# The first block's value weights: eight load slots, an earlier first split, three low halves on GpSimd, and later low halves of the values

## The chip, the cores and the metric

The kernel runs on one core of one Trainium2 chip. The metric is the device time of one execution in microseconds; of several executions the median counts. In the views, PE is TensorE's matmul row, PEld its weight loads, DVE VectorE, ACT ScalarE, POOL GpSimd, and SP the engine whose queue issues most DMAs.

## The reference

A transformer layer over two sequences of 2048 tokens with 2048 channels: layer norm, single-head attention with 512 features, and a routed low-rank feed-forward part, both added to the input.

```python
xn = layernorm(x)                                   # per token, over 2048 channels
q, k, v = split(xn @ Wqkv + bqkv)                   # 512 features each
att = softmax(q @ k.T / sqrt(512)) @ v @ Wo + bo
s = (xn @ Wq_w.T) @ keys.T                          # router, 16 dimensions, 64 experts
gate = softmax over the 16 largest of s, 0 elsewhere
z = (xn @ A_w.T).reshape(64, 8) * gate[:, None]     # 8 columns for each expert
out = x + att + (z @ B_w.T) * 2
```

All is float32.

## The kernel before

**Numbers in two halves.** The operands of the products are of type fp32r. Every one is split in two: the high half is a cast copy (`split_hi`, a cast on ScalarE, line 121), the low half is what is missing (`split_lo`, a subtraction on VectorE, line 124). `product` (line 129) then does three matmuls: low token half by high weight half, high by low, high by high.

**Blocks.** The 4096 tokens are eight blocks of 512, each of four token tiles of 128 rows. The first block is made by `first_block`, before anything else; this change is in it alone. Other blocks and the attention follow, and are not touched.

**What the first block does.** For each token tile t it loads 128 rows (`load`, line 340), takes the row statistics on VectorE (`normal`: lines 200, 203, then nm at 348 and, in `rstd`, ve at 193 and a power on GpSimd at 194 that gives rs), scales the rows (`scale`: three quarters on VectorE at 356, one on ScalarE at 360 and 361), transposes them on TensorE (`turn`, line 370, 16 transposes in four groups, each group into one accumulator), and splits the transposed group into high and low halves (xh, lines 121 and 124). Then come the products with the value weights. The values (with the 16 router columns) are 528 columns wide and are made in two halves h of 264 columns. The weights of one half come in eight pieces of 128 by 528 numbers (two channel chunks of 264), each of 264 KB, loaded at line 270 into a slot ws, and split into wh. One token tile with one piece takes six matmuls, of 128 by 264.

**The order.** In the first half, the products go tile by tile: 36 matmuls of tile 0 (pieces 1 to 6), transposes of tile 1, tile 0's other 12 and 48 of tile 1, transposes of tile 2, 48, transposes of tile 3, 48. In the second half they go piece by piece, each with all four tiles, which is 24 matmuls for a piece. Between these, `values_out` splits each tile's sum into vs (a cast on ScalarE, a subtraction on VectorE that reads the accumulator) and stores it (line 163, through `flush`).

**What sets the order.** Each engine runs its instructions in one order that is fixed when the program is built, by a scheduler. `behind(keys)` puts what is inside it after the last instruction that was noted under these names ("row" is the last row or token operation of VectorE). A `Ring` gives out named buffers in turn, and an instruction that fills one waits until the former content has been read. Here matter: `r_ws` (four slots h0 to h3 for loaded value weights), `r_mb` (B25, B26), `r_wu` (seven slots, B32 and B33 the last two, for query, key and feed-forward weights), `r_ev` (three slots, for vs among others), and the seven accumulators `acc` in PSUM, which are given to transposed groups and to sums alike.

In the first block, `pieces(n)` loads and splits pieces until n are there:

```python
        turn(0, 0, 2)
        pieces(2)
        turn(0, 2, 4)
        pieces(4)
        load(1, 1024)
```

and two more are asked for at the start of tile 0's products, and the last two in the midst of them.

Of the kernel before, what the change touches and what calls it, by code (L numbers as in the profile page):

```python
# [8 lines left out]
F32 = mybir.dt.float32  # L9
# [7 lines left out]
P = 128  # L17
# [10 lines left out]
VH = (D + RD) // 2  # L28
# [5 lines left out]
def raw(ap):  # L34
    return ap.bitcast(F32)
# [27 lines left out]
def attn_ffn_kernel(ctx: ExitStack, tc, x, xT, wq, wv, wob, bqk, bv, bo, keysT, out):  # L63
    nc = tc.nc
# [10 lines left out]
    sb = ctx.enter_context(tc.tile_pool(name="sb", bufs=1))  # L75
# [5 lines left out]
    def big(*js):  # L81
        return Ring(sb, *(f"B{j}" for j in js))
# [4 lines left out]
    def half(*js):  # L87
        return Ring(sb, *(f"H{j}" for j in js))

    def mid(*js):  # L90
        return Ring(sb, *(f"h{j}" for j in js))
# [6 lines left out]
    def acc():  # L98
        return psum.tile([P, T], F32, name="acc", tag="acc", bufs=7)
# [11 lines left out]
    def behind(*keys):  # L111

        ctx_ = ExitStack()
        for k in keys:
            ctx_.enter_context(tc.issue_after(last[k].ins))
        return ctx_

    def split_hi(hi, src):  # L120
        return nc.scalar.copy(hi, src)  # L121

    def split_lo(lo, src, hi, eng=None):
        return (eng or nc.vector).tensor_tensor(lo, src, raw(hi), ALU.subtract)  # L124
# [33 lines left out]
    def store(dst, src):  # L158
        pending.append((dst, src))
# [10 lines left out]
    r_ev = big(27, 28, 29)  # L170
# [3 lines left out]
    r_ws = mid(0, 1, 2, 3)  # L174
# [21 lines left out]
    def row_stats(mv, xs, parts, st):  # L196

        for xt in xs:
            for h in range(xt.shape[1] // 512):
                nc.vector.bn_stats(st[:, parts, :], xt[:, h * 512 : (h + 1) * 512])  # L200
                parts += 1
        if parts == 4:
            nc.vector.bn_aggr(mv, st)
        return parts
# [60 lines left out]
            xn.append(xh)  # L265
        return xn

    def weights(src, shape, eng=None, queue=None):
        ws = r_ws([P, *shape], F32, "ws")
        issued = (queue or nc.sync).dma_start(ws, src)  # L270
        if queue is None:
            last["sp"] = issued
        wh = r_wh([P, 2, *shape], FR, "wh")
        last["hi"] = split_hi(wh[:, 0], ws)
        last["dve"] = split_lo(wh[:, 1], ws, wh[:, 0], eng)
        return wh

    def values_out(i, t, h, r, qr, ps, u=None):

        n0 = RD if h == 0 else 0  # L280
        at = 0 if h == 0 else VH - RD
        vs = r([P, 2, VH], FR, "vs")
        if u is None:
            v = ps
            if h == 0:
                nc.scalar.copy(qr[:, t, :RD], ps[:, :RD])
        else:
            v = raw(vs[:, 1, :])
            nc.vector.tensor_tensor(v[:, n0:], ps[:, n0:VH], u[:, n0:], ALU.add)
        last["ev"] = split_hi(vs[:, 0, n0:], v[:, n0:VH])  # L290
        split_lo(vs[:, 1, n0:], v[:, n0:VH], vs[:, 0, n0:])
        store(v_d[i][t][:, :, at : at + VH - n0], raw(vs[:, :, n0:]))

    def wv_piece(h, c2, eng=None, queue=None):
        ch, cc = divmod(2 * c2, HC)
        return weights(wv[h, ch, :, cc : cc + 2, :], [2, VH], eng, queue)

    def router_in():
        qr = const.tile([P, NT, 32], F32, name="qr", bufs=1)
# [26 lines left out]
    def first_block():  # L326


        xs0 = [r_xs, r_xs, r_xs] + [big(j) for j in range(16, 21)]
        xn = [r_xh([P, 2, T], FR, "xh") for c in range(NCH)]  # L330
        rows, mv = {}, const.tile([P, NT, 2], F32, name="mv", bufs=2)
        rs = const.tile([P, NT], F32, name="rs")
        nm = const.tile([P, NT], F32, name="nm")

        def load(t, cols):
            rows[t] = [xs0[2 * t + c]([P, 1024], F32, "xs") for c in range(2)]
            for c in range(2):
                for h in range(1024 // cols):
                    a = h * cols
                    (nc.scalar if t == 0 and c else nc.sync).dma_start(  # L340
                        rows[t][c][:, a : a + cols],
                        x[t * P : (t + 1) * P, c * 1024 + a : c * 1024 + a + cols],
                    )

        def normal(t):
            st = const.tile([P, 4, 6], F32, name="st6", bufs=2)
            row_stats(mv[:, t, :], rows[t], 0, st)
            last["nm"] = nc.vector.tensor_scalar(nm[:, t : t + 1], mv[:, t, 0:1], -1.0, None, ALU.mult)
            rstd(rs[:, t : t + 1], mv[:, t, 1:2], 1)

        def scale(t):
            for n in range(4):
                c, h = divmod(n, 2)
                v = rows[t][c][:, h * 512 : (h + 1) * 512]
                if n < 3:
                    last["row"] = nc.vector.tensor_scalar(
                        v, v, mv[:, t, 0:1], rs[:, t : t + 1], ALU.subtract, ALU.mult
                    )
                else:
                    nc.scalar.activation(v, v, AF.Identity, bias=nm[:, t : t + 1])  # L360
                    last["mul"] = nc.scalar.mul(v, v, rs[:, t : t + 1])

        def turn(t, g0=0, g1=NCH // 4):
            sl = slice(t * P, (t + 1) * P)
            for g in range(g0, g1):
                pt = acc()
                for j in range(4):
                    c = 4 * g + j
                    k = (c % 8) * P
                    nc.tensor.transpose(pt[:, j * P : (j + 1) * P], rows[t][c // 8][:, k : k + P], ident)  # L370
                for part in range(2):
                    for j in range(4):
                        hi, lo = (xn[4 * g + j][:, a, sl] for a in range(2))
                        pj = pt[:, j * P : (j + 1) * P]
                        if part == 0:
                            split_hi(hi, pj)
                        else:
                            last["row"] = split_lo(lo, pj, hi)

        def piece(c2, h, eng=None, queue=None):  # L380
            return wv_piece(h, c2, eng, queue)

        def mul(ps, wh, t, c2):
            sl = slice(t * P, (t + 1) * P)
            for cc in range(2):
                c = 2 * c2 + cc
                product(
                    ps[:, :VH], lambda a: xn[c][:, a, sl], lambda b: wh[:, b, cc, :],
                    c == 0, c == NCH - 1,
                )  # L390

        N2 = NCH // 2
        warm = half(0)([P, T], mybir.dt.bfloat16, "warm")
        nc.vector.memset(warm, 0.0)
        pw = misc()
        for j in range(26):
            nc.tensor.matmul(pw, warm[:, :P], warm, start=True, stop=True)
        load(0, 512)
        normal(0)
        scale(0)  # L400

        wh = []

        def pieces(n):
            with behind("row", "nm", "mul"):
                while len(wh) < n:
                    wh.append(piece(len(wh), 0))

        turn(0, 0, 2)
        pieces(2)  # L410
        turn(0, 2, 4)
        pieces(4)
        load(1, 1024)
        ps = [acc() for t in range(NT)]
        for t in range(NT):
            if t + 1 < NT:
                with behind("row"):
                    normal(t + 1)
            if t == 0:
                pieces(6)  # L420
                load(2, 1024)
            for c2 in range(N2):
                if t + 1 < NT and c2 == 2:
                    scale(t + 1)
                if t == 0 and c2 == 4:
                    pieces(N2)
                    load(3, 1024)
                    constants()
                if t + 1 < NT and c2 == 6:
                    with behind("pe"):  # L430
                        turn(t + 1)
                mul(ps[t], wh[c2], t, c2)
        qr = router_in()
        for t in range(NT):
            values_out(0, t, 0, r_ev, qr, ps[t])
        flush()
        ps = [acc() for t in range(NT)]
        for c2 in range(N2):
            w = piece(c2, 1)
            for t in range(NT):  # L440
                mul(ps[t], w, t, c2)
        for t in range(NT):
            values_out(0, t, 1, r_ev, qr, ps[t])
        return xn, qr
# [120 lines left out]
    def value_sums(m, w):  # L565
# [21 lines left out]
    pieces = [  # L587
        (j, ph, it, g)
        for j in PAIRS for ph in PHASES for it in ITEMS[ph] for g in range(2 if it == "V" else 1)
    ]  # L590
# [386 lines left out]
    xn, qr = first_block()  # L977
    tile_of = lambda fp, fh: ND * (fp // 2) + 2 * fh + fp % 2
    for i in range(2):
        if i:  # L980
            s2 = stats_steps(2, r_xs, 1024, mbs)
            qr = values(i, xn, s2)
# [54 lines left out]
    r_ev = big(27, 28, 29, 9)  # L1037
# [544 lines left out]
    for q in range(2 * NG):  # L1582
# [4 lines left out]
        for n, step in enumerate(STEPS):  # L1587
# [7 lines left out]
            for t in range(NA):  # L1595
                ps = multiply(q, step, t, bank.get(t) if step == "P2" else None)
# [58 lines left out]
```

## Time and profile before

| what | value |
|---|---|
| three runs | 2624.99, 2626.7, 2631.52 us; median 2626.7 |
| profiled execution: its own time | 2629.96 us |
| its span in the profile | 2628.2 us |
| TensorE's granted clock, mean | 0.997 |
| first block: loads of value weights, one piece | 264 KB, 3.8 us from issue to landing (median of 20) |
| first block: loads of rows, half a tile | 512 KB, 8.7 us (median of 6) |
| VectorE: low half of a weight piece, 128 by 528 | 0.70 us |
| VectorE: low half of a transposed chunk, 128 by 128 | 0.28 us, one each 0.2 us |
| ScalarE: high half of a weight piece | 0.62 to 0.83 us |
| VectorE: statistics of a tile, four operations | 2.46 us |
| TensorE: 16 transposes | 2.0 us |

A row of the timeline gives the start in the span, the length, the engine, the line of the kernel, the operation with out<-in, the shape and how many were merged; in brackets the time for which the engine stood idle just before, and what ended that. Instructions of one engine overlap at their ends, so several in a row start closer together than their lengths say. A row "min/median/max" gives durations in ns. In a row of the windows, the stretch and its length come first, then the busy time of each engine.

### The profile page before, as it was taken

To read this page: it belongs to the slowest core of one execution; us is meant where nothing else is said; L and a number is where in the kernel's file an instruction comes from. 1 tells how busy PE (TensorE), PEld (TensorE's weight loads), DVE (VectorE), ACT (ScalarE), POOL (GpSimd) and SP (SyncE) were. 2 spreads that over 40 slices of the span, in tenths; PEclk is the share of its full clock that TensorE was granted. 3 is DMA by queue.
4 is the path that set the end of the run, shared out by engine and by line. 5 is a ranking of instruction groups with operands and counts; after the bars stand their busy time and mean duration, and the time that the engine had idled before them with its cause. 6 is when DMAs were issued, how large, how long until landed. Compare 5 with 4: busy or idle time off the path is not lost. (4 is left out here: it accounts for less than half of the span.)

```text
span 2628.2 us, 34501 instructions
## 1 busy us (share of the span) xinstructions
PE 2592.6 (99%) x12692; PEld 2186.3 (83%) x12692; DVE 1919.4 (73%) x2698; ACT 909.8 (35%) x1345; POOL 516.1 (20%) x315
## 2 busy tenths in 40 slices
PE   8999999999999999999989999999999999999999
PEld 7889888888888888888877877878888888888887
DVE  7557639867878677776758859678598776797675
ACT  4323223323332333343435436344364222332221
POOL 1311420000000000000000000000000765566654
PEclk9999999999999999999999999999999999999999
DMA  6667875668447683576999798799788544565542
GB/s 235 232 248 261 284 262 186 211 211 278 153 136 226 214 274 124 177 257 226 310 305 326 253 329 268 257 331 321 251 294 296 175 164 161 183 217 176 177 162 103
DMA packets 328954, 608.09 MB, mean 231 GB/s; under 512 B 27928, under 2 KB 150864, under 8 KB 328784
## 3 DMA queue, kind: packets, MB, share of 16 engines
q1 hardware_dynamic: 315824, 575.99, 64.9%
q10 hardware_dynamic: 12960, 29.89, 3.4%
q8 instruction: 100, 1.64, 0.3%
q14 instruction: 70, 0.57, 0.1%
HBM read 450.42 MB, written 155.35 MB: 230 GB/s over the span
## 5 line engine op out<-in xcount | busy, mean ns | idle before, releaser
L129 PE MATMUL acc<-t,pw 128*128 128x512 f32 x3024 | 694.0, 390 | 1.6 <-DVE pw L124 1.5
L129 PEld LDWEIGHTS acc<-t,pw 128*128 128x128 f32 x3024 | 565.3, 188 | 119.7 <-DVE pw L124 2.5
L1406 PE MATMUL acc<-wb,s 128*128 128x512 f32 x2688 | 609.4, 389 | 0.0
L1406 PEld LDWEIGHTS acc<-wb,s 128*128 128x128 f32 x2688 | 504.5, 188 | 104.8
L1390 POOL TENSOR_TENSOR xo<-xo,bo_bc 128x512 f32<-128x512 f32 x128 | 205.6, 1613 | 906.4 <-DMA vt<-v_d 606.2
L129 PE MATMUL acc<-ph,vt 128*128 128x512 f32 x1536 | 378.6, 391 | 4.5 <-DVE ot L1255 2.5
L1129 PE MATMUL acc<-qt,kt 128*128 128x512 f32 x1344 | 338.4, 394 | 14.3 <-ACT acc L1112 7.4
L129 PEld LDWEIGHTS acc<-ph,vt 128*128 128x128 f32 x1536 | 287.7, 188 | 68.5 <-DVE ot L1255 4.1
L1129 PEld LDWEIGHTS acc<-qt,kt 128*128 128x128 f32 x1344 | 253.1, 190 | 73.7 <-ACT acc L1112 8.3
L121 ACT CAST pw<-pw 128x1024 fp32r<-128x1024 f32 (+1 forms) x168 | 177.6, 1058 | 324.8 <-PE acc L129 240.9
L129 PE MATMUL acc<-xh,wh 128*128 128x512 f32 x1152 | 263.7, 390 | 0.0
L124 DVE TENSOR_TENSOR pw<-pw 128x1024 fp32r<-128x1024 f32 (+1 forms) x168 | 214.7, 1278 | 64.9 <-ACT pw L121 63.5
L129 PEld LDWEIGHTS acc<-xh,wh 128*128 128x128 f32 x1152 | 215.6, 188 | 44.9
L129 PEld LDWEIGHTS acc<-pw,t 128*128 128x128 f32 x2016 | 245.8, 188 | 1.3
L129 PE MATMUL acc<-pw,t 128*128 128x264 f32 x2016 | 246.4, 283 | 0.0
L121 ACT CAST s<-xz 128x1024 fp32r<-128x1024 f32 x112 | 118.0, 1054 | 368.7 <-PE acc L1406 285.8
L124 DVE TENSOR_TENSOR s<-xz,s 128x1024 fp32r<-128x1024 f32 x112 | 175.4, 1568 | 41.6 <-ACT s L121 41.6
L124 DVE TENSOR_TENSOR wh<-wu,wh 128x512 fp32r<-128x512 f32 x96 | 83.6, 888 | 99.0 <-ACT wh L121 99.0
L519 POOL TENSOR_TENSOR zt<-zt,g 128x512 f32<-128x512 f32 x24 | 38.9, 1630 | 503.3 <-DMA g<-gd 272.4
L121 ACT CAST t<-xq 128x1024 fp32r<-128x1024 f32 x84 | 88.3, 1052 | 103.5 <-PE acc L129 44.8
L124 DVE TENSOR_TENSOR t<-xq,t 128x1024 fp32r<-128x1024 f32 x84 | 108.2, 1292 | 20.6 <-ACT t L121 20.1
L1395 DVE TENSOR_TENSOR xo<-xo,acc 128x512 f32<-128x512 f32 x128 | 86.8, 679 | 49.1 <-PE acc L1406 22.3
(168 smaller groups left out, 2463.2 us busy)
## 6 DMA issues: line engine op xcount, KB each, us to landing
vt<-v_d SPq DMA_DIRECT2D x128, 512.0 KB, 5.3
kt<-kp_d SPq DMA_DIRECT2D x224, 256.0 KB, 5.8
pw<-sq_d SPq DMA_DIRECT2D x72, 512.0 KB, 4.0
xo<-in_x SPq DMA_DIRECT2D x128, 256.0 KB, 3.4
xz<-oz_d SPq DMA_DIRECT2D x64, 512.0 KB, 4.8
out_y<-xo SPq DMA_DIRECT2D x128, 256.0 KB, 2.3
pw<-in_wq SPq DMA_DIRECT2D x54, 512.0 KB, 4.4
wu<-in_wq SPq DMA_DIRECT2D x48, 512.0 KB, 5.9
```

What stands on the lines that cost most here:

```text
L121: return nc.scalar.copy(hi, src)
L124: return (eng or nc.vector).tensor_tensor(lo, src, raw(hi), ALU.subtract)
L129: last["pe"] = nc.tensor.matmul(ps, st(a_), mv(b_), start=first and n == 0, stop=end and n == 2)
L519: nc.gpsimd.tensor_tensor(zt, zt, gx[n], ALU.mult)
L1129: last["pe"] = nc.tensor.matmul(ps, st[:, d, a, :], mv[c][:, d, :], start=not more and d == 0 and i == 0, stop=d == 1 and i == 2, skip_gro ...
L1390: nc.gpsimd.tensor_tensor(xs, xs, bo_bc[q // (NB // 2 * NH), c], ALU.add)
L1395: nc.vector.tensor_tensor(xs, xs, ps, op)
L1406: nc.tensor.matmul(ps, st[a_][:, kk, sl], mv[b_], start=not more and kk == 0 and n == 0, stop=kk == ND - 1 and n == 2, skip_group_check=more,)
```

## The change

Four things are changed, all in the first block:

- The first half's eight pieces get a ring of their own, `r_w0`, with eight slots: the four of `r_ws`, and B25, B26, B32 and B33. The second half's pieces use `r_ws` as before.
- The first piece is asked for ahead of the first transposes, two more after the first two groups, two more after the others.
- The low halves of the third, fourth and fifth piece are subtracted on GpSimd.
- The values of the first half are split and stored behind "row", which then is the last token operation of the fourth tile.

```diff
-    def weights(src, shape, eng=None, queue=None):
-        ws = r_ws([P, *shape], F32, "ws")
+    def weights(src, shape, eng=None, queue=None, ring=None):
+        ws = (ring or r_ws)([P, *shape], F32, "ws")
...
-        def piece(c2, h, eng=None, queue=None):
-            return wv_piece(h, c2, eng, queue)
+        r_w0 = Ring(sb, "h0", "h1", "h2", "h3", "B25", "B26", "B32", "B33")
...
         def pieces(n):
             with behind("row", "nm", "mul"):
                 while len(wh) < n:
-                    wh.append(piece(len(wh), 0))
-
+                    eng = nc.gpsimd if 2 <= len(wh) < 5 else None
+                    wh.append(wv_piece(0, len(wh), eng, ring=r_w0))
+
+        pieces(1)
         turn(0, 0, 2)
-        pieces(2)
+        pieces(3)
         turn(0, 2, 4)
-        pieces(4)
+        pieces(5)
         load(1, 1024)
...
         qr = router_in()
         for t in range(NT):
-            values_out(0, t, 0, r_ev, qr, ps[t])
+            with behind("row"):
+                values_out(0, t, 0, r_ev, qr, ps[t])
         flush()
         ps = [acc() for t in range(NT)]
         for c2 in range(N2):
-            w = piece(c2, 1)
+            w = wv_piece(1, c2)
```

`wv_piece` passes the ring on to `weights`.

More of the change, by code (lines that the diff above doesn't have):

```diff
@@ L292, in values_out, with wv_piece @@
         store(v_d[i][t][:, :, at : at + VH - n0], raw(vs[:, :, n0:]))
-    def wv_piece(h, c2, eng=None, queue=None):
+    def wv_piece(h, c2, eng=None, queue=None, ring=None):
         ch, cc = divmod(2 * c2, HC)
-        return weights(wv[h, ch, :, cc : cc + 2, :], [2, VH], eng, queue)
+        return weights(wv[h, ch, :, cc : cc + 2, :], [2, VH], eng, queue, ring)
     def router_in():
```

## The prediction

> **What bounds the kernel now.** I read the page's busy shares first: TensorE is busy for almost the whole span, so a change pays only where TensorE stands still, or where it makes it stand still.
>
> ```profile
> PE 2592.6 (99%) x12692; PEld 2186.3 (83%) x12692; DVE 1919.4 (73%) x2698; ACT 909.8 (35%) x1345; POOL 516.1 (20%) x315
> ```
>
> The change touches only the first block, so the second view is the timeline of TensorE in the first 60 us (start, length, operation, idle time before it and its releaser):
>
> ```profile
> 9.18 2.00 PE L370 MATMUL acc<-ident,xs 128*128 128x128 f32 x16 [0.20 <-DVE xs L356]
> 11.02 0.39 PE L129 MATMUL acc<-wh,xh 128*128 128x264 f32 x1
> 13.11 1.70 PE L129 MATMUL acc<-wh,xh 128*128 128x264 f32 x12 [1.70 <-DVE wh L124]
> 15.84 1.97 PE L129 MATMUL acc<-wh,xh 128*128 128x264 f32 x12 [1.03 <-DVE wh L124]
> 20.00 1.61 PE L129 MATMUL acc<-wh,xh 128*128 128x264 f32 x11 [2.19 <-DVE wh L124]
> 21.45 1.91 PE L370 MATMUL acc<-ident,xs 128*128 128x128 f32 x16
> ...
> 30.71 2.01 PE L370 MATMUL acc<-ident,xs 128*128 128x128 f32 x16
> 32.79 6.11 PE L129 MATMUL acc<-wh,xh 128*128 128x264 f32 x48
> 41.25 2.00 PE L370 MATMUL acc<-ident,xs 128*128 128x128 f32 x16 [2.36 <-issue]
> 43.07 17.17 PE L129 MATMUL acc<-wh,xh 128*128 128x264 f32 x139
> ```
>
> Rows of 16 are the transposes of one token tile (I call their starts T0 9.18, T1 21.45, T2 30.71, T3 41.25). Three waits of 4.92 us together are for low halves of weights (wh, from VectorE), and one of 2.36 us stands before T3. From 43.07 on there is no gap: the windows show 20.00 us busy in each 20 us from 60 to 180. So the place where the fourth tile's products start, 43.07, is the number to move; the four gaps, 7.28 us, are all there is to win.
>
> The third view is VectorE's timeline of the same time:
>
> ```profile
> 10.68 1.67 DVE L124 TENSOR_TENSOR xh<-acc,xh 128x128 fp32r<-128x128 f32 x8 [0.64 <-ACT xh L121]
> 12.27 1.31 DVE L124 TENSOR_TENSOR wh<-ws,wh 128x528 fp32r<-128x528 f32 x2
> 15.09 1.31 DVE L124 TENSOR_TENSOR wh<-ws,wh 128x528 fp32r<-128x528 f32 x2
> 16.32 2.46 DVE L200 BATCH_NORM_STATS2 st<-xs 128x6 f32<-128x512 f32 x4
> 19.25 1.32 DVE L124 TENSOR_TENSOR wh<-ws,wh 128x528 fp32r<-128x528 f32 x2
> 20.48 1.45 DVE L356 TENSOR_SCALAR xs<-xs,mv,rs 128x512 f32<-128x512 f32 x3
> 39.41 0.42 DVE L124 TENSOR_TENSOR vs<-acc,vs 128x248 fp32r<-128x248 f32 x1 [1.02 <-ACT vs L121]
> 40.61 1.46 DVE L356 TENSOR_SCALAR xs<-xs,mv,rs 128x512 f32<-128x512 f32 x3 [0.66 <-POOL rs L194]
> ```
>
> VectorE is full from 10.68 to 23: weights' low halves stand ahead of the statistics of the next tile. At 38.38 it stops for a value row (vs) whose products end only then; the fourth tile's statistics wait behind it. That is the cause of the 2.36 us named "issue".
>
> [...]by lines 194 and 549:
>
> ```profile
> L194 POOL TENSOR_TENSOR rs<-ve,nhalf x4: 548/558/956, 8.0 to 40.0; 128x1 f32<-128x1 f32 x4
> L549 POOL TENSOR_TENSOR ws<-ws x4: 1321/1328/8414, 58.4 to 350.6; 128x528 f32<-128x528 f32 x4
> ```
>
> The 956 ns one starts at 19.41, beside two wh operations of VectorE (two SBUF inputs); the other three have none beside them. [...]here 1.32 (up to 1.66 in line 550) against 0.70 us. [...]
>
> **The change part by part.** I follow the chain to T1, T2, T3. The order of each engine's instructions is that of the built program.
>
> *Ahead of T1, loads.* The eight slots let SP issue pieces 5 to 8 without waiting for a low half. Before, ScalarE waited 4.5 us for three of them. SP moves piece 5 (264 KB) ahead of tile 1's rows and piece 6 ahead of tile 2's: at the about 0.4 MB/us of this time, tile 1 lands 0.7 us later. Issued at about 4.5 with the row's 8.7 us to landing, that is 13.9; the statistics want it at 14.7, so it costs nothing, but by under 1 us. Tiles 2 and 3 land by 20 and are wanted at 24 and 34.
>
> *VectorE up to the statistics.* Pieces 3 and 4 go to GpSimd: 15.09 to 16.32, 1.23 us, gone. Piece 1's low half moves into the 0.64 us idle before 10.68: 0.61 gone. ScalarE now casts piece 3 ahead of the second eight token casts (0.54 to 0.62), so VectorE's second eight start at 13.1, not 12.9: 0.2 back. Statistics start at 16.32 - 1.84 + 0.2 = 14.7.
>
> *GpSimd.* Piece 3's low half is ready at 12.4[...]; it runs 13.0 to 14.3. Piece 4's cast ends at 14.3: 14.4 to 15.75. Piece 5: to 17.1 (17.7 at 1.66 each). The rs of tile 1 stands behind them on GpSimd, and is asked for at 19.33 - 1.6 = 17.7. So they fit, just.
>
> *T1.* VectorE does piece 6's low half 17.65 to 18.35; rs is [...]done at 18.75, as 956 ns before. Scale 18.8 (before 20.48); its first quarter, 0.54 us, allows T1 at **19.4**. TensorE: piece 6's six matmuls at 0.126 us (7.55/60 in the row of 60 after 23.11) end at 19.1. T1 moves by 2.05 us.
>
> *T2.* Scale, then pieces 7 and 8, then xh as before: xh at 21.45 (1.65 earlier). Statistics to T2 took 4.45 us; a value low half (0.31 of queue) leaves the gap: 24.6 + 4.14 = 28.75. TensorE itself is ready at 19.4 + 9.21 = 28.6. T2 at **28.75**, 1.95 earlier.
>
> *T3.* T2 to T3 was 10.54 us. The value low half's 1.02 wait and 0.33 of pitch go: 9.2, T3 at **37.95**, 3.3 earlier. What is late next is VectorE's chain still: TensorE ends tile 2 at about 36.8.
>
> *The fourth tile.* The three value low halves now stand after its sixteen xh operations, so three accumulators stay unread. With four for the transposes all seven banks are taken, and the fourth tile's first product must wait until VectorE has read the first transposed group: by the program it waits for the fourth xh operation instead of the first. Three operations of 0.2 us pitch: 0.6 us. Start at 37.95 + 1.82 + 0.6 = **40.35**, against 43.07.
>
> *Behind it.* Three value low halves, 1.2 us, now precede the second half's weights on VectorE: first one ready at 44.5, wanted at 40.35 + 6.1 = 46.4. Three value stores, 0.6 us each on SP, go from 29 to 40 us to about 43.5, ahead of the loads of second-half pieces 5 to 8 (3.8 us to landing, so by 53); piece 5 is wanted after four pieces of 24 matmuls, 58.6. The fourth value cast on ScalarE waits for the first store to land (4.1 us, to 47.6), and queues weight casts of piece 5 behind it. The products hide all this with about 5 us to spare. The last two slots are buffers of the query weights' ring; their loads now wait for pieces 7 and 8 (21.4), before they are due.
>
> **Sum.** 43.07 - 40.35 = 2.7 us. Against the profiled execution's 2629.96 that is 2627.3; that execution was 3.3 above the median of three, so I predict 2626.7 - 2.7 = **2624.0**.
>
> Costs that the trace before does not show: GpSimd's three subtractions with an fp32r output, 1.32 to 1.66 each (I take 1.32; the other end costs up to 0.3 by way of rs); [...]the bank wait, 0 to 0.9 us[...]. From 3.5 to 0.8 us gained.
>
> **Rivals.**
> [...]VectorE's piece 2 waits for 1.3 us and all after it. For: the margin is about 0.15 us. Against: VectorE's start hangs on its own queue, GpSimd's on a ScalarE cast that ends later. Gain 1.4: 2625.3.
> *Hidden later.* TensorE's next wait over 2 us, 7.23 us before a key product at 1331, could take the gain back. Against: its releaser is a ScalarE copy of TensorE's own last result, so it moves along. Gain 0: 2626.7.
> *Slower: GpSimd starves.* Line 549 has one subtraction of 8.41 us, among dense two-input VectorE work. If one of the three is held so, rs comes 7.1 us later, T1 at 26.5, 5 us after the 21.45 of before; 0.7 of the later steps is still won: 4.3 slower, 2631.0; two of them 2638. It decides from 2.7 us of extra delay in GpSimd's three. Against: between 13 and 17.6 VectorE works on PSUM or one input.
> *It does not do what it says:* the built order has all moves where I count them.
>
> **How the numbers follow.** Main course 0.70, [...]hidden 0.10, starved 0.06. 0.3% is 7.9 us, about what a measurement of this kernel can tell from no change; the three runs shown spread over 6.5 us. Even all four gaps do not reach it, so faster by over that, 0.03, is scatter alone; slower, 0.03, needs two starved operations or scatter. The range takes 3.5 to 0 us of gain and about 3 us of scatter between two medians: 2620.3 to 2627.6.
>
> **What would show it.** Right: three L124 rows on POOL of 1.3 to 1.7 us; statistics at 14.7; T1, T2, T3 near 19.4, 28.75, 37.95; no vs row before 42 on VectorE; products of the fourth tile from 40.3, then no gap to 180. Wrong: a POOL row over 3 us; a wh row of VectorE over 1 us at 12.3; T1 after 20.7; a new gap between 46 and 66; or the same early start with the span unchanged.

## The result, and the profile after

| | before | after |
|---|---|---|
| median of 22 executions each, side by side | 2631.19 us | 2626.49 us |
| lowest and highest | 2624.99, 2636.59 | 2620.38, 2633.61 |
| ratio of the executions, 95% interval | | 0.9985 [0.9978, 0.9992] |
| profiled execution | 2629.96 us | 2625.36 us |
| from the first transpose to the fourth tile's products | 33.89 us | 31.21 us |

The ratio is a gain of 3.9 us of 2631, between 2.1 and 5.8. The time lies in the predicted range. A later set of 17 executions of the changed kernel gave 0.9978 [0.9969, 0.9987], 5.8 us, between 3.4 and 8.2. The forecast gain, 2.7 us, is inside the first interval but below its centre, and below the whole of the second; that excess is what most of the experiments are about.

The busy shares of the page after hardly differ from those of before; three operations have moved from VectorE's count to GpSimd's.

```profile
PE 2592.8 (99%) x12692; PEld 2186.1 (83%) x12692; DVE 1921.8 (73%) x2695; ACT 909.8 (35%) x1345; POOL 528.2 (20%) x318
```

The timeline of TensorE after, first 62 us:

```profile
9.35 1.91 PE L370 MATMUL acc<-ident,xs 128*128 128x128 f32 x16
11.14 1.26 PE L129 MATMUL acc<-wh,xh 128*128 128x264 f32 x7
13.14 0.99 PE L129 MATMUL acc<-wh,xh 128*128 128x264 f32 x6 [0.74 <-DVE wh L124]
14.32 1.00 PE L129 MATMUL acc<-wh,xh 128*128 128x264 f32 x6 [0.19 <-POOL wh L124]
15.82 1.00 PE L129 MATMUL acc<-wh,xh 128*128 128x264 f32 x6 [0.51 <-POOL wh L124]
17.10 1.00 PE L129 MATMUL acc<-wh,xh 128*128 128x264 f32 x6 [0.28 <-POOL wh L124]
18.46 0.88 PE L129 MATMUL acc<-wh,xh 128*128 128x264 f32 x5 [0.36 <-DVE wh L124]
19.47 2.01 PE L370 MATMUL acc<-ident,xs 128*128 128x128 f32 x16
21.23 7.55 PE L129 MATMUL acc<-wh,xh 128*128 128x264 f32 x60
28.92 2.00 PE L370 MATMUL acc<-ident,xs 128*128 128x128 f32 x16
...
38.02 2.01 PE L370 MATMUL acc<-ident,xs 128*128 128x128 f32 x16 [1.00 <-DVE xs L356]
40.55 21.69 PE L129 MATMUL acc<-wh,xh 128*128 128x264 f32 x176 [0.53 <-DVE xh L124]
```

Before, the three stands for wh were 1.70, 1.03 and 2.19 us; now five are 0.19 to 0.74, three of them for GpSimd. The 2.36 us before the last transposes are 1.00. A new wait of 0.53 us stands before the fourth tile's products: the accumulator that the prediction put at 0.6. From there on TensorE is busy without a gap, 20.00 us in each 20 us of the windows from 60 to 180.

The listed gaps fall from 7.28 to 3.61 us, by 3.67, while the products of the fourth tile start only 2.68 us earlier in their distance from the first transpose. The rows show most of the difference: six products that follow a wait take 1.00 us, where sixty in a row take 0.126 each, 0.76 for six. The starts of the single products in the trace say what these 0.24 us are. In such a six the second product starts 0.23 us after the first, and the others 0.12 us apart, as in the long row; the last one ends 0.28 us after its start, while in an unbroken row the next would have started 0.12 us after it. So about 0.1 us is a slower start after a wait, and the rest, about 0.16 us, is waiting that the list does not count, because a gap is counted only from the end of the last product. The changed kernel waits seven times and the kernel before four, so the sum of gaps overstates the gain; the start of the next unbroken stretch does not.

VectorE and GpSimd of the same time, from their timelines after:

```profile
12.38 0.70 DVE L124 TENSOR_TENSOR wh<-ws,wh 128x528 fp32r<-128x528 f32 x1
13.20 1.68 DVE L124 TENSOR_TENSOR xh<-acc,xh 128x128 fp32r<-128x128 f32 x8
14.79 2.46 DVE L200 BATCH_NORM_STATS2 st<-xs 128x6 f32<-128x512 f32 x4
...
17.71 0.70 DVE L124 TENSOR_TENSOR wh<-ws,wh 128x528 fp32r<-128x528 f32 x1
18.87 1.46 DVE L356 TENSOR_SCALAR xs<-xs,mv,rs 128x512 f32<-128x512 f32 x3 [0.46 <-POOL rs L194]
...
42.79 1.05 DVE L124 TENSOR_TENSOR vs<-acc,vs 128x248 fp32r<-128x248 f32 x3
```

```profile
12.57 1.70 POOL L124 TENSOR_TENSOR wh<-ws,wh 128x528 fp32r<-128x528 f32 x1 [4.44 <-ACT wh L121]
14.44 2.60 POOL L124 TENSOR_TENSOR wh<-ws,wh 128x528 fp32r<-128x528 f32 x2 [0.18 <-ACT wh L121]
17.88 0.96 POOL L194 TENSOR_TENSOR rs<-ve,nhalf 128x1 f32<-128x1 f32 x1 [0.83 <-DVE ve L193]
```

GpSimd's first low half starts at 12.57, inside VectorE's wh of 12.38 to 13.08, and takes 1.70 us; the next two, beside VectorE operations on PSUM and the statistics, take 1.30 each. The rs at 17.88 meets VectorE's wh of 17.71 and takes 0.96 us as before. No vs row comes before 42.79.

### The profile page after: what moved, and what is told of

It is laid out like the page before. It is cut to its first block, busy times and chain, and to the rows that moved or that the text cites. A ratio compares the mean times of both kernels' runs of the same rounds, so it can differ in the third digit from the quotient of the medians.

```text
span 2623.5 us, 34496 instructions
## 1 busy us (share of the span) xinstructions
PE 2592.8 (99%) x12692; PEld 2186.1 (83%) x12692; DVE 1921.8 (73%) x2695; ACT 909.8 (35%) x1345; POOL 528.2 (20%) x318
## 5 line engine op out<-in xcount | busy, mean ns | idle before, releaser
L1131 PE MATMUL acc<-qt,kt 128*128 128x512 f32 x1344 | 338.0, 393 | 14.3 <-ACT acc L1114 7.6
L124 DVE TENSOR_TENSOR t<-xq,t 128x1024 fp32r<-128x1024 f32 x84 | 108.2, 1292 | 20.1 <-ACT t L121 19.7
```

The lines of the kernel that those rows point to most:

```text
L1131: last["pe"] = nc.tensor.matmul(ps, st[:, d, a, :], mv[c][:, d, :], start=not more and d == 0 and i == 0, stop=d == 1 and i == 2, skip_gro ...
```

## Experiments

Below, "the distance" is that from the start of the first transpose to the fourth tile's products, the number that the prediction was about.

### The parts, one at a time

**The values' low halves alone**, on the kernel before:

```diff
         for t in range(NT):
-            values_out(0, t, 0, r_ev, qr, ps[t])
+            with behind("row"):
+                values_out(0, t, 0, r_ev, qr, ps[t])
```

> The kernel before, with the fourth part of the change alone: the first half's values are split behind the last token operation of the fourth tile. Measure: from the first transposes (T0) to the fourth tile's first product, 33.9 us before and 31.2 after. Theory (the value row held up the fourth tile's statistics by 1.35 us, and the held accumulators cost 0.6): T3 comes 1.35 earlier, the gap before T3 of 2.36 becomes about 1.0, a new gap of 0.5 to 0.6 stands before the fourth tile's products; 33.1 us in all. Rival (the gap named 'issue' has another cause, the statistics themselves): the gap before T3 stays over 2 us; 33.9 or, with the bank wait, 34.5.

Measured: 2631.83 us, distance 34.65. The two waits are as expected, in the timeline of TensorE:

```profile
19.98 2.79 PE L129 MATMUL acc<-wh,xh 128*128 128x264 f32 x11 [1.72 <-DVE wh L124]
22.57 2.19 PE L370 MATMUL acc<-ident,xs 128*128 128x128 f32 x16
...
41.32 2.01 PE L370 MATMUL acc<-ident,xs 128*128 128x128 f32 x16 [1.00 <-DVE xs L356]
43.86 2.33 PE L129 MATMUL acc<-wh,xh 128*128 128x264 f32 x17 [0.54 <-DVE xh L124]
```

From the third tile's transposes to the fourth's it is 9.41 us (10.54 before), then 2.54 instead of 1.82: a gain of 0.4 in these rows. But the distance is longer than before, not shorter: eleven products at 19.98 took 2.79 us, where before they took 1.61. The worth of this part cannot be read from the distance as it stands; the cause is looked for below.

**All but the values**: the changed kernel without its `behind("row")`.

> The changed kernel without the fourth part: values are split where they were before. Theory (the parts add): T1 and T2 as after the change, T2 at most 0.3 later; the gap before T3 of about 2.4 us is back and the gap before the fourth tile's products gone; from T0 to the fourth tile's products about 32.2 us. Rival (the gains of the weight parts and the value part overlap, one of them would do): under 31.6 us.

Measured: 2621.74 us, distance 33.01, 0.8 longer than expected. The first transposes to the second are 10.13 us, as in the changed kernel (10.12; before 12.27), so this part is the whole of that step, and the 2.36 us before the last transposes are back. The excess lies in one row, the last transposes:

```profile
38.87 3.28 PE L370 MATMUL acc<-ident,xs 128*128 128x128 f32 x16 [2.36 <-issue]
41.80 4.47 PE L129 MATMUL acc<-wh,xh 128*128 128x264 f32 x31
```

Sixteen transposes took 3.28 us instead of 2.0. Neither the theory's 32.2 nor the rival's "under 31.6" was measured.

**The low halves back from GpSimd to VectorE**: the changed kernel with

```diff
-                    eng = nc.gpsimd if 2 <= len(wh) < 5 else None
+                    eng = None
```

> The changed kernel with the low halves of pieces 3 to 5 on VectorE again; slots, early first piece and late values stay. Theory (VectorE's queue ahead of tile 1's statistics sets T1): three low halves of 0.61 us pitch are back ahead of the statistics, which start near 16.6 instead of 14.8, T1 near 21.3, from T0 to the fourth tile's products about 33.0 us. Rival (the loads' waits for slots were the cause, so the slots carry the gain): statistics may be late, but T1 stays under 20.2 and the stretch under 31.7 us.

Measured: 2629.39 us, distance 34.05, 1.0 longer than expected, so a miss in that number. The rest came as the theory had it: statistics start at 16.51 (14.79 in the changed kernel), the second tile's transposes at 21.46, not under 20.2, and the wh waits are 0.73, 1.09 and 2.44 us. Here too, products and transposes ran long from 20.2 us on.

**The old ring of four slots**: the changed kernel with

```diff
-        r_w0 = Ring(sb, "h0", "h1", "h2", "h3", "B25", "B26", "B32", "B33")
+        r_w0 = r_ws
```

> The changed kernel with the first half's pieces in the old ring of four slots; everything else stays. Theory (VectorE's queue is the bound; the loads are hidden): piece 5's load waits for piece 1's low half, near 10.1, and tile 1's rows behind it on SP until then; they land near 14.5, the statistics start within 0.5 us of 14.8, T1 by 20.1; stretch from T0 to the fourth tile's products 31.2 to 31.9 us. Rival (the slots carry much of the gain): tile 1's statistics start after 16, T1 after 20.7 and the stretch is over 32.3 us.

Measured: 2626.91 us, distance 33.03, over the 31.9 of the theory. The statistics are not late (14.13, 5.50 us after the first transpose; 5.44 in the changed kernel), which speaks for the theory; the fifth piece's products wait 0.99 us instead of 0.28, since its load waits for a slot. The rest of the excess is again rows that ran long, from 18.3 us.

### What ran long: the granted clock

The trace records the granted clock of TensorE, and the windows average it. In these four kernels it falls to half for 3.41 us in the first block: from 19.7 in the first, 39.4 in the second, 20.2 in the third, 18.3 in the fourth. The windows of the first two, on both sides of the fall (stretch, its length, busy time of PE, PEld, DVE, ACT, POOL with their counts, granted clock, DMA share, GB/s):

```profile
16.30:19.70 3.40, 1.51 (x11) 1.10 (x9) 3.33 (x9) 1.68 (x3) 0.31 (x1) 1.00 0.95 324
19.70:23.10 3.40, 3.12 (x14) 3.12 (x15) 3.40 (x7) 2.09 (x4) 0.65 (x1) 0.50 0.56 165
```

```profile
36.00:39.40 3.40, 1.04 (x10) 0.78 (x9) 1.72 (x6) 1.88 (x4) 0.55 (x1) 1.00 0.71 267
39.40:42.80 3.40, 3.40 (x17) 3.40 (x17) 2.68 (x13) 2.93 (x16) 0.00 (x0) 0.50 0.86 240
```

In both, TensorE had stood for more than half of the 3.4 us ahead. The profile of before, from which I predicted, has no such stretch.

With the rows that ran at half put back to the lengths that they have in the kernels before and after, the four distances come to about 33.3, 31.9, 33 and 31.5 us, where the theories had 33.1, 32.2, 33.0 and 31.2 to 31.9. That is an estimate, good to about 0.3 us. By it, of the 2.7 us the held-back values are worth 0.6 to 0.7, the move of three low halves to GpSimd nearly 2, and the eight slots a few tenths. The earlier first piece was in all of these kernels but the first, and was not tried alone.

Both kernels were run once more.

> The kernel before, unchanged, profiled once more, to see how far places in the profile repeat. Theory (the first block is set by its own chain): T0 to the fourth tile's products 33.9 us within 0.2; the gaps of 1.70, 1.03, 2.19 and 2.36 us in their places within 0.2. Rival (they are scatter of the loads): some differ by over 0.5 us. For the rest of the span: if the 1.5 us gap at about 407 us and the sum of gaps after 1350 differ from the first profile by over 1 us, what the two profiles differ by there is scatter.

> The changed kernel, unchanged, profiled once more. Theory: T0 to the fourth tile's products 31.2 us within 0.2, three GpSimd rows of 1.3 to 1.7 us. Rival [...]: a low half of VectorE near 12.4 of over 1 us, and the stretch over 32 us.

The kernel before: 2630.55 us, distance **35.96**, and half clock from 14.3 to 24.6:

```profile
10.90:14.30 3.40, 1.70 (x14) 1.45 (x13) 3.40 (x14) 3.40 (x15) 0.00 (x0) 1.00 1.03 422
14.30:24.60 10.30, 8.48 (x38) 7.87 (x38) 8.92 (x22) 4.80 (x11) 0.96 (x1) 0.50 0.79 250
```

The changed kernel: 2623.35 us, distance 31.18, no half clock in the first block. So the distance of the same kernel before is 33.9 us in one profile and 36.0 in the other. It did not repeat within the expected 0.2 us: the profile that I used was one of the good executions. That of the changed kernel did repeat.

The clock record of the traces shows a step. Every stretch at 0.5 (but the last, which the end of the kernel cuts) is 3.41, 6.83 or 10.24 us, one to three times 3.41, and the stretches at full clock between them fit the same step: in the kernel before, 177.49 and 1109.33 us are 52 and 325 times 3.413. The phase, the place of these borders against the kernel's start, differs between executions: the first falls at 5.29 us in the profile of before and at 6.36 in that of after. So I read the record as windows of 3.41 us. No window of the first block was idle (the emptiest was busy for 0.29). I laid the windows over TensorE's busy time, in all 14 profiles of this study, from 7.4 to about 50 us, wherever the clock was full:

| TensorE's busy share of the window | windows | clock half in the next |
|---|---|---|
| 0.29 to 0.44 | 3 | 3 |
| 0.46 to 0.60 | 12 | 2 |
| over 0.60 | 146 | 0 |

The rest of these 14 profiles says the same, and adds how the clock comes back. Over whole kernels, all 26 windows that were busy for less than 0.45 were followed by half clock, 5 of the 38 from 0.45 to 0.60, and 1 of some 10600 above. At half clock, all 21 windows up to 0.81 busy were followed by another at half, and all 32 from 0.92 by a full one. So in these profiles the clock came back only after a window that was busy for at least 0.92, and a stretch got long where TensorE still waited: in the three windows of the 10.24 us above TensorE was busy for 0.81, 0.66 and 1.00.

In the kernel before, each of the stands of 1.7 to 2.4 us can bring a window to about half or below, depending on the phase: 0.50 at 12.1 us and 0.46 at 39.4 in its first profile, with full clock after both, and 0.50 at 10.9 in its second, with half clock after it. The same busy times with the windows laid at every phase, and 0.5, my choice from the table above, as the limit, give 1.6 such windows in the kernel before on average and none in the changed kernel, whose worst window is busy for 0.58. That is an estimate, and 0.5 is no sharp limit: one of the windows followed by half clock, that of the changed kernel with four slots, was busy for 0.60.

### Filling the stands of the kernel before

If that is so, work that does nothing should make the kernel before faster.

```diff
+        def idle(n):
+            for j in range(n):
+                nc.tensor.matmul(pw, warm[:, :P], warm, start=True, stop=True)
...
                 mul(ps[t], wh[c2], t, c2)
+                if t == 0 and c2 in (1, 3):
+                    with behind("pe"):
+                        idle(3 if c2 == 1 else 9)
```

> The kernel before, with twelve more of the dummy bf16 matmuls of line 397 (0.21 to 0.30 us each) put into TensorE's two longest stands of the first token tile: three after the second piece's products (a stand of 1.03 us there, 0.66 in the second profile of it) and nine after the fourth's (2.19 us). The order on VectorE and ScalarE is unchanged. Theory of the clock (TensorE's granted clock falls to half for 3.4 or 10.2 us when it stands too much in the first block, and this costs the kernel before 1 to 2 us in some of its executions, over and above its waits): in the profile no stretch at half clock ahead of 40 us, and from the first transpose to the fourth tile's products the 33.9 us of the undisturbed profile of the kernel before, or up to 0.3 more where a dummy delays a product; as half to all executions of the kernel before lose 1 to 2 us so, a time 0.5 to 2 us below it. Rival (the half-clock stretches come by themselves, whatever TensorE stands): a stretch at half clock here too, in five profiles of six as with the old waits, and a time equal to the kernel before or up to 0.3 us above it.

Measured: 2626.46 us (21 executions) against 2630.37 for the kernel before (46), ratio 0.9985 [0.9976, 0.9994]: **3.9 us faster, between 1.6 and 6.3**. The distance in its profile is 33.86 us, as in the good execution of before, and the clock is full. (The 2.36 us ahead of the last transposes are not filled; by the estimate above, 0.7 windows are still at half or below, so in other executions the clock may fall there.)

```profile
14.84 0.59 PE L398 MATMUL misc<-warm 128*128 128x512 bf16 x2
...
15.93 1.61 PE L129 MATMUL acc<-wh,xh 128*128 128x264 f32 x11 [0.37 <-DVE wh L124]
17.38 2.12 PE L398 MATMUL misc<-warm 128*128 128x512 bf16 x9
...
20.09 1.61 PE L129 MATMUL acc<-wh,xh 128*128 128x264 f32 x11 [0.48 <-DVE wh L124]
21.54 1.91 PE L370 MATMUL acc<-ident,xs 128*128 128x128 f32 x16
```

```profile
13.10:16.50 3.40, 2.86 (x18) 2.37 (x20) 3.40 (x12) 1.24 (x4) 0.00 (x0) 1.00 1.00 400
16.50:19.90 3.40, 3.12 (x19) 1.81 (x17) 3.33 (x8) 1.76 (x3) 0.39 (x1) 1.00 0.96 318
```

No wait of the first tile was removed: real products start where they started before (13.20, 15.93, 20.09; before 13.11, 15.84, 20.00). What changed is that TensorE was busy meanwhile. The mean granted clock is listed for every execution, so this rests on more than one profile: 0.99687 for the 46 executions of before, 0.99781 for the 21 here (standard errors up to 0.0002). The difference, 0.00094 of 2628 us, is at most 2.5 us of work at full clock, and that agrees with the lower half of the interval. The rival, that the stretches come by themselves, expected the same clock and no gain, and that does not fit; that the clock was won in the first block and nowhere else is seen in one profile only. The centre of the measurement, 3.9, is above the 2 us that I expected at most, and the interval does not let me say by how much. The profiled execution itself was a late one, 2636.53 us: TensorE stood 3.52 us at 396.6 in a later block, which the edit does not touch, and the clock was half for the 6.8 us from 398.8. The window ahead of that fall was busy for 0.36.

### The changed kernel again, and its last wait

> The changed kernel once more, timed beside the three others on one chip. If its advantage is the 2.7 us of waits plus the half-clock stretches of the kernel before, 3 to 5 us below it, and no half-clock stretch in the first block of its profile; if the half clock has no part in it, 2.7 us below it, give or take what the measurement scatters.

Measured: 2624.03 us (17 executions), ratio 0.9978 [0.9969, 0.9987]; no half clock in the first block, distance 31.25. On the same chip its median is 2.4 us below that of the filled kernel before, near the 2.6 us by which their distances differ (33.86 and 31.25). That alone proves little: from the executions on record the means differ by 2.0 us, with a 95% interval from -0.3 to 4.3. Its mean clock is 0.99824, above before by 0.00137, at most 3.6 us.

**The wait for an accumulator**: in the changed kernel

```diff
-            with behind("row"):
+            with behind("nm" if t < 2 else "row"):
                 values_out(0, t, 0, r_ev, qr, ps[t])
```

so that the values of tiles 0 and 1 are split after the last row statistics, and their accumulators come free before the last transposes.

> The changed kernel, but the values of tiles 0 and 1 are split behind the fourth tile's statistics (nm) instead of behind its last token operation; those of tiles 2 and 3 as after the change. Theory (the 0.53 us gap before the fourth tile's products is the wait for an accumulator): two accumulators come free before T3, the gap goes; the two value rows of VectorE fall into its idle time of 0.66 and 0.74 us there; from T0 to the fourth tile's products 30.6 to 30.8 us instead of 31.2. Rival (VectorE's queue is so full that each value row costs its 0.33 us): T3 is 0.3 to 0.7 later and the stretch 31.2 to 31.6 us.

Measured: 2619.44 us, distance 30.68, as the theory had it, and the wait of 0.53 us gone. That confirms what the wait is for. Whether it is worth anything was then timed:

> The changed kernel with the values' low halves of tiles 0 and 1 held only behind the last row statistics and those of tiles 2 and 3 behind the fourth tile, timed. If the stand of 0.53 us ahead of the fourth tile's products is the price of holding all four back, and what is won there reaches the end: 0.5 us below the changed kernel, so 3.5 to 5.5 us below the kernel before. If later waits take it back: equal to the changed kernel. One profile of it ended at 2619.4 us, 4 to 6 us below those of the changed kernel; of this the first block explains 0.5, so I expect the rest to be scatter of the later blocks and not to come again.

Measured: 2625.46 us (14 executions), ratio 0.9978 [0.9967, 0.9988]. In TensorE's timeline the fourth tile's products follow the transposes without a wait:

```profile
38.09 2.01 PE L370 MATMUL acc<-ident,xs 128*128 128x128 f32 x16 [1.00 <-DVE xs L356]
40.13 6.07 PE L129 MATMUL acc<-wh,xh 128*128 128x264 f32 x48
```

The distance is 0.4 to 0.5 us shorter, in two profiles (30.68 and 30.78); in time it cannot be told from the changed kernel. It is not a version that I can call better.

**More on GpSimd**: the changed kernel with `2 <= len(wh) < 8`, the low halves of pieces 3 to 8.

> The changed kernel with six low halves on GpSimd, pieces 3 to 8, instead of three. Theory (rs of tile 1 stands in GpSimd's queue, and a low half there takes 1.3 us): piece 6 runs to 18.4 and rs after it, rs itself 0.55 us because no two-input operation of VectorE is beside it; T1 19.5 to 19.7; pieces 7 and 8 end near 21.5 and 22.8, so tile 0's last products wait 0.5 to 0.8 us; stretch from T0 to the fourth tile's products 31.5 to 32.0 us, worse than with three. Rival (VectorE is the bound everywhere, each operation moved off it gains 0.6 us): T2 and T3 earlier, stretch under 31.0 us.

Measured: 2627.97 us, distance 32.58, longer than the 31.2 of the changed kernel and than expected. The second tile's transposes start no earlier in distance (10.13 us), although VectorE is freed of one more low half: the second tile's rs now stands behind four low halves on GpSimd, until 17.72, and the transposes wait 0.23 us for the rows that it scales. A later piece comes late too (0.28 us at 22.29), and the third tile's transposes are interrupted by a wait of 0.45 us for ScalarE's quarter of the row:

```profile
22.29 6.72 PE L129 MATMUL acc<-wh,xh 128*128 128x264 f32 x53 [0.28 <-POOL wh L124]
...
30.77 0.66 PE L370 MATMUL acc<-ident,xs 128*128 128x128 f32 x4 [0.45 <-ACT xs L361]
```

Three on GpSimd is enough here; six loses 1.4 us of distance.

### Another place with half clock

Every profile so far has a second place: at the start of the attention scores TensorE stands 4.6 to 8.2 us for ScalarE (the expectation below says 7.4 at most; one kernel, the held-back values alone, has 8.17). In the changed kernel:

```profile
1324.00:1328.00 4.00, 0.00 (x0) 0.00 (x0) 3.92 (x12) 2.57 (x7) 0.00 (x0) 0.50 0.06 24
1328.00:1334.00 6.00, 5.76 (x14) 4.50 (x15) 1.62 (x5) 1.91 (x5) 0.00 (x0) 0.50 0.82 265
```

```diff
             score(g)
+            if g == 1:
+                with behind("pe"):
+                    pz = misc([P, P])
+                    for j in range(34):
+                        nc.tensor.transpose(pz, ident, ident)
```

> The changed kernel with 34 dummy transposes of the identity (0.125 us each when they follow one another, 4.3 us in all) on TensorE at the start of the attention scores, behind their first 13 matmuls, where TensorE stands 4.6 to 7.4 us for ScalarE in every profile so far, and where each profile shows the clock at half for 6.8 or 10.2 us. In the changed kernel's profile the half clock there lasts from 1323.9 to 1334.1 us, and the work starts at 1328.2, so 5.9 us of work run at half: 2.9 us lost (2.2 and 2.8 in two more profiles of it). Theory of the clock: the stand is left at 0.4 to 3.1 us, no stretch at half clock shows there or one of 3.4 us at most, and the time falls by 1.5 to 2.9 us against the changed kernel, so 6 to 8.5 us below the kernel before where the changed kernel was 4 to 6 below it. Rival (the clock falls there by itself, or falls from something other than TensorE standing): the half-clock stretch stays, and the time is that of the changed kernel, or later by what a dummy holds up.

Measured: 2625.67 us (12 executions), ratio 0.9982 [0.9972, 0.9991]. The timeline of TensorE there:

```profile
1320.89 3.87 PE L1529 MATMUL misc<-ident 128*128 128x128 f32 x34
1327.67 8.66 PE L1131 MATMUL acc<-qt,kt 128*128 128x512 f32 x30 [2.91 <-ACT acc L1114]
```

A stand of 2.91 us is left, and the half clock is one window of 3.41 us (from 1327.6) instead of two or three. The mean clock is 0.99875, against 0.99824 of the changed kernel, which was timed on another chip. But the time is that of the changed kernel: the 6 to 8.5 us below the kernel before were not reached, the ratio is worth 4.7, and only their lower part lies inside the interval (2.4 to 7.4). So filling shortens the half clock at this place too, and whether the time follows there stays open. By the profiles of the two kernels 1.2 us was to be had (work at half: 5.9 us before, 3.4 now), which these 12 executions could not show.

## Why the prediction was right, and what it left out

- **Statistics and T1.** Predicted 14.7 and 19.4, measured 14.79 and 19.47. GpSimd's three operations did what the prediction chose: VectorE's wh started first, at 12.38, and the first low half ended at 14.27 (14.3 predicted), the last at 17.04 (17.1). That GpSimd's would wait for VectorE's end was my estimate. Measured, the one that started first kept its length and the other took longer: VectorE's wh 0.70 us and GpSimd's low half 1.70 against 1.30. In the kernel before, at 58.4 us, the order is the other way: GpSimd's subtraction took its 1.32 us, and VectorE's wh 1.65, against 0.69 for one of the same shape with nothing on GpSimd beside it (55.70):

```profile
58.39 1.32 POOL L549 TENSOR_TENSOR ws<-ws 128x528 f32<-128x528 f32 x1 [17.82 <-DMA ws<-in_wv]
58.62 1.65 DVE L124 TENSOR_TENSOR wh<-wu,wh 128x512 fp32r<-128x512 f32 x1 [2.23 <-ACT wh L121]
```

- **T2, T3, the fourth tile.** Predicted 28.75, 37.95 and 40.35, measured 28.92, 38.02 and 40.55, in an execution that began 0.17 later (9.35, not 9.18). The accumulator wait, taken as 0.6, was 0.53, and holding back two of the four values instead removed it.
- **Behind it.** The stores of the values left SP from 43.26, as forecast, and TensorE had no gap in the second half.
- **The rivals.** No GpSimd operation starved: the longest was 1.70 us. That VectorE's work on PSUM or one input would not hold GpSimd up was my estimate; beside such work the other two took 1.30 us each. The gain was not hidden later, as far as profiles show. From the first transpose to the start of the stand ahead of the attention scores it is 1314.9 us in the kernel before and 1311.9 in the changed kernel's second profile, 3.0 less. Neither has half clock in between, and both have one stand of 1.5 us near 405. The rows from which this is taken, first the kernel before:

```profile
1331.28 9.51 PE L1129 MATMUL acc<-qt,kt 128*128 128x512 f32 x30 [7.23 <-ACT acc L1112]
1326.62 9.15 PE L1131 MATMUL acc<-qt,kt 128*128 128x512 f32 x30 [5.25 <-ACT acc L1114]
```

- **The step that was mis-sized** is the sum. "Four gaps, 7.28 us, are all there is to win" counts time in which TensorE stands, and takes for granted that it runs at full speed in between. In the kernel before it does not always: the same stands also cost it the clock, 2.1 us in its second profile (35.96 against 33.89), and, over many executions, 1.6 to 6.3 us by the time of the fill and at most 2.5 by its clock. The prediction had no term for this; its mean clock of 0.997 was in the table, and was not followed to its place, because in the one profile shown that place was not in the first block. With about 2 us for it the sum would be 4.7, which lies in both measured intervals.
- **The base, and luck.** The three executions shown had a median of 2626.7; 22 give 2631.19. So the predicted time came out 2.5 us below the measured one although the gain was larger than predicted, and the two errors partly cancel. That the time lies in the range is luck: from a base of 2631.19 the forecast gain leads to 2628.5, above the range's end of 2627.6. That end does not follow from the terms given for it either: no gain and 3 us of scatter from 2626.7 make 2629.7.
- **A misread wait.** Of the 4.5 us that ScalarE waited for loads before, only 3.55, in two waits, lie ahead of the second tile's transposes; the third, 0.97 at 51.68, is for a piece of the second half. Nothing in the sum rests on it.

The runs leave open how the excess over 2.7 us divides between the clock and scatter. After 1300 us the gaps of one and the same kernel differ by about 4 us between two profiles (18.4 and 14.7 us in all from 1300 to 1800 for the kernel before), so two single executions decide nothing below that.

## What to carry to other kernels

In this kernel, with TensorE busy for 99% of the span, stands of 1.0 to 2.4 us cost their own length in one profile and 2.1 us more in clock in another (33.89 and 35.96 us); so look at the granted clock of several profiles before pricing a gap, and lay the gaps over the steps that the clock record shows, here 3.41 us. Many short waits in place of a few long ones gained less than the list of gaps says (here each wait cost about 0.24 us beside its listed gap) but kept the clock at full in the first block, in all three profiles of the changed kernel. To tell lost clock from lost time, fill the stand with dummy matmuls: here that alone made the kernel 3.9 us faster (1.6 to 6.3) and its mean clock higher (0.99781 against 0.99687), which points to the clock.

## What the hardware showed that I had not expected

- The clock was halved after windows in which TensorE was still busy for 29 to 60% of the time, in stretches of 3.41 or 10.24 us; no gap in the first block was as long as such a stretch (the longest 2.44 us). It came back only after windows that were busy for at least 92%.
- Twelve matmuls whose result nothing uses made a kernel 3.9 us faster (1.6 to 6.3).
- A GpSimd subtraction of 128 by 528 with an fp32r output took 1.30 us beside VectorE work on PSUM and statistics, and 1.70 where it met VectorE's two-input operation for 0.5 us: the meeting cost 0.4 us, and no more.
